# Latent attention of a hybrid layer stack: the softmax denominators of one batch are added on DVE, copies out of PSUM move to ACT, and the end of the first half runs between products of the second

## The chip, the cores and the metric

The kernel runs on one core of one Trainium2 chip. A core has five engines with a queue of their own each: PE (TensorE, matrix products into PSUM), DVE (VectorE), ACT (ScalarE), POOL (GpSimd) and SP (SyncE, which issues DMAs here). An instruction waits at the head of its engine's queue until what it needs is there, and everything behind it waits too. The metric is the device time in microseconds (us) of one execution of the whole kernel.

## The reference, cut to what matters

The kernel computes two layers of mixed blocks on `x` of shape 2 x 1024 x 128 (batch, rows, width), all in float32. Only the first block is touched, a causal attention with 16 heads whose keys and values come out of a latent of 32 numbers per row:

```python
q_blhd = jnp.einsum('bld,dhk->blhk', x_bld, Wq)
latent_bll = jnp.einsum('bld,dc->blc', x_bld, Wkv_down)
k_blhd = jnp.einsum('blc,chk->blhk', latent_bll, Wk_up)
v_blhd = jnp.einsum('blc,chk->blhk', latent_bll, Wv_up)
attn = jnp.einsum('bqhd,bkhd->bhqk', q_blhd, k_blhd) / jnp.sqrt(jnp.asarray(HD, dtype=x_bld.dtype))
mask = (jnp.arange(l)[None, :] <= jnp.arange(l)[:, None])[None, None]
attn = jax.nn.softmax(jnp.where(mask, attn, neg_inf), axis=-1)
y_blhd = jnp.einsum('bhqk,bkhd->bqhd', attn, v_blhd)
return jnp.einsum('bqhd,hdo->bqo', y_blhd, Wout)
```

After it come, for each batch, a spiking feed-forward, a state-space block (a scan along the rows), a linear attention, experts, another attention and experts again.

## The kernel before

The key matrices are folded into the queries and the value matrices into the output, so that each head works on the latent itself: scores are products of 32 numbers, and the weighed sum of a head has 32 numbers per row. Four heads fill the 128 rows of PE's array; the 16 heads are four *chunks* `c` of four heads `j`. Rows are taken in two *halves* of 512 queries; keys in blocks `kb` of 128. A half needs the key blocks 0 to 3, or 0 to 7, and of the four blocks on the diagonal only the queries from the block on: 512, 384, 256 and 128 columns. One pair (c, kb) is a *unit*: 16 units in the first half, 32 in the second, the last four of each chunk diagonal, the others full.

A unit, in `LatentAttention.attend` (L265), has two parts. `exponentials` (L274): four score products of one head each (L282, "scores"), four products that add the negative row maximum to them (L291, "addm"), into two PSUM tiles `a_st` of two heads each; two exponentials on ACT (L301, 1024 elements a row for a full unit) into SBUF tiles `a_pT`, of which there are six; and for a diagonal unit a mask on GpSimd for each tile (L304, `affine_select`). `weigh` (L313): four products with the latent, summed over a chunk's units in the PSUM bank `a_oT` (L320, "weighing"), and four products with ones, summed over a whole half in the bank `a_dT` (L328, "denominators"). At a chunk's last unit DVE copies `a_oT` into SBUF, `a_oU` (L336). The step that computes the exponentials of one unit weighs the unit before.

The *end* of a half follows its last unit: DVE's reciprocal of the denominators (L348), for each chunk a product that spreads them over the rows ("pick", L352) and DVE's multiplication of `a_oU` with it (L353), and for each of four row blocks four output products (L358) that DVE adds to the residual `x_res` (L362). Picks and outputs use `a_st` tiles as well.

Batch 0 runs alone: `first_layer` drains `attend(0)` (three `a_st` tiles of two banks, `a_oT` and `a_dT` one bank each, eight banks in all), and there a scheduler orders each engine's instructions by times that it estimates. Then the maxima of batch 1 (L225, L243) are woven with batch 0's feed-forward (`spiking_steps`, whose norm has a square root on ACT, L66), and `attend(1)`, with two `a_st` tiles, with batch 0's state-space loop: inside `tc.manual_schedule` each engine takes its instructions in the order in which the program writes them. The loop has 32 steps of two loads, a decay on ACT (L606) and three DVE instructions (L637, L638 the scan, L639); `weave` takes 1.75 steps of the generator `attend(1)`, that is as many `yield`s, for each step of the loop:

```python
        attend = latent.attend(1, work, ps, ps_o)
        with tc.tile_pool(name="s_work", bufs=1, reuse_waits="tile") as work:
            weave(space[0].loop(work, bank), attend, 1.75)
        drain(attend)
```

Of the kernel before, what the change touches and what calls it, by code (L numbers as in the profile page):

```python
# [9 lines left out]
F32 = mybir.dt.float32  # L10
BF16 = mybir.dt.bfloat16
AF = mybir.ActivationFunctionType
ALU = mybir.AluOpType
# [4 lines left out]
ALL = {ENG.PE, ENG.DVE, ENG.Activation, ENG.Pool, ENG.SP}  # L18

P = 128  # L20
B = 2
L = 1024
D = 128
NT = B * L // P
TPB = L // P
# [3 lines left out]
class Ctx:  # L29


    def __init__(self, ctx, tc, dram):
        nc = tc.nc
        self.nc, self.tc, self.dram = nc, tc, dram
        self.const = ctx.enter_context(tc.tile_pool(name="const", bufs=1))
        self.small = ctx.enter_context(tc.tile_pool(name="small", bufs=4))
        self.x = self.const.tile([P, NT, D], F32, name="x_res")
        self.ident = self.const.tile([P, P], F32, name="ident")
        make_identity(nc, self.ident)
        self.eps = self.const.tile([P, 1], F32, name="eps")  # L40
        nc.vector.memset(self.eps, EPS)
# [46 lines left out]
def drain(steps):  # L88
    for _ in steps:
        pass  # L90
# [20 lines left out]
class LatentAttention:  # L111
# [3 lines left out]
    C, J, LD = 4, 4, 32  # L115
# [146 lines left out]
        nc.vector.tensor_copy(self.nmT[b], pt.rearrange("p a b -> p (a b)"))  # L262
        yield

    def attend(self, b, work, ps, ps_o):  # L265
        g, nc, C, J = self.g, self.g.nc, self.C, self.J
        qT, latT, lat, nmT = self.qT[b], self.latT[b], self.lat[b], self.nmT[b]
        for half in range(2):
            kbs = list(range(4 * half + 4))
            dT = ps_o.tile([P, 512], F32, name="a0_dT")  # L270
            oU = work.tile([P, C, 512], F32, name="a0_oU")
            oTs = {}

            def exponentials(c, kb):  # L274

                off = max(kb * P - half * 512, 0)
                q0 = half * 512 + off
                n = 512 - off
                ss = [ps.tile([P, 2, 512], F32, name="a0_st") for _ in range(2)]
                for j in range(J):  # L280
                    quad = slice(32 * j, 32 * j + 32)
                    nc.tensor.matmul(  # L282
                        ss[j // 2][:, j % 2, off:],
                        latT[quad, bass.ts(kb, P)],
                        qT[quad, c, q0 : q0 + n],
                        start=True,
                        stop=False,
                    )
                for j in range(J):
                    quad = slice(32 * j, 32 * j + 32)  # L290
                    nc.tensor.matmul(  # L291
                        ss[j // 2][:, j % 2, off:],
                        self.addm[quad, c, :],
                        nmT[quad, q0 : q0 + n],
                        start=False,
                        stop=True,
                    )
                pTs = []
                for s in ss:
                    pT = work.tile([P, 2, 512], F32, name="a0_pT", bufs=6)  # L300
                    nc.scalar.activation(pT[:, :, off:], s[:, :, off:], AF.Exp)  # L301
                    if kb * P >= half * 512:
                        diag = pT[:, :, off : off + P]
                        nc.gpsimd.affine_select(  # L304
                            out=diag,
                            in_=diag,
                            pattern=[[0, 2], [1, P]],
                            compare_op=ALU.is_ge,
                            fill=0.0,
                            base=0,  # L310
                            channel_multiplier=-1,
                        )
                    pTs.append(pT)  # L313
                return pTs, off

            def weigh(c, kb, pTs, off):
                if kb == 0:
                    oTs[c] = ps_o.tile([P, 512], F32, name="a0_oT")
                for j in range(J):
                    nc.tensor.matmul(  # L320
                        oTs[c][32 * j : 32 * j + 32, off:],
                        lat[:, kb, :],
                        pTs[j // 2][:, j % 2, off:],
                        start=(kb == 0),
                        stop=(kb == kbs[-1]),
                    )
                for j in range(J):
                    nc.tensor.matmul(  # L328
                        dT[32 * j : 32 * j + 32, off:],
                        self.ones[:, c, :],  # L330
                        pTs[j // 2][:, j % 2, off:],
                        start=(c == 0 and kb == 0),
                        stop=(c == C - 1 and kb == kbs[-1]),
                    )
                if kb == kbs[-1]:
                    nc.vector.tensor_copy(oU[:, c, :], oTs.pop(c))  # L336

            units = [(c, kb) for c in range(C) for kb in kbs]
            held = {}
            for step in range(len(units) + 1):  # L340
                if step < len(units):
                    held[step] = exponentials(*units[step])
                if step >= 1:
                    weigh(*units[step - 1], *held.pop(step - 1))
                yield

            rec = work.tile([P, 512], F32, name="a0_rec")
            nc.vector.reciprocal(rec, dT)  # L348
            yield
            for c in range(C):  # L350
                rr = ps.tile([P, 2, 512], F32, name="a0_st")
                nc.tensor.matmul(rr[:, 0, :], self.pick[:, c, :], rec, start=True, stop=True)  # L352
                nc.vector.tensor_mul(oU[:, c, :], oU[:, c, :], rr[:, 0, :])  # L353
            yield
            for i in range(4):
                pf = ps.tile([P, 2, 512], F32, name="a0_st")
                for c in range(C):
                    nc.tensor.matmul(  # L358
                        pf[:, 0, :D], oU[:, c, bass.ts(i, P)], self.wvo[:, c, :], start=(c == 0), stop=(c == C - 1)
                    )  # L360
                xt = g.x[:, b * TPB + 4 * half + i, :]
                nc.vector.tensor_add(xt, xt, pf[:, 0, :D])  # L362
            yield

# [829 lines left out]
def first_layer(g, w, open_experts, load_expert):  # L1196

    tc = g.tc
# [12 lines left out]
    with ExitStack() as es:  # L1211
        latent.project([pool(es, "a0_batch0", 1), own])
        with tc.tile_pool(name="a0_seq", bufs=1) as seq, tc.tile_pool(name="a0_ps_a", bufs=2, space=PSUM) as ps:
            drain(latent.row_maxima(0, seq, ps, 4))
        work = pool(es, "a0_work", 2)
        ps, ps_o = pool(es, "a0_ps_b", 3, space=PSUM), pool(es, "a0_ps_o", 1, space=PSUM)
        drain(latent.attend(0, work, ps, ps_o))

    bank = banks(spaces, "bank", 2)
    shared = StateConstants(g, w, pool(spaces, "s_one", 1))  # L1220
# [25 lines left out]
    with tc.manual_schedule(engines=ALL):  # L1246
# [7 lines left out]
        work = pool(latents, "a0_work", 1, **right)  # L1254
# [133 lines left out]
```

## Time and profile before

| | |
|---|---|
| time, median of 3 runs | 2319.74 us (2317.05 to 2331.03) |
| the profiled execution's own time | 2328.53 us |
| its span, first to last instruction | 2326.8 us |
| mean granted PE clock | 0.931 |
| busy: PE, DVE, ACT, POOL | 87%, 70%, 51%, 37% of the span |
| attention of batch 0, half 0, its end, half 1, its end | 147.8 to 198, to 211, to 305, to 319.5 us |
| attention of batch 1, woven with the state-space loop: half 0, its end, half 1, its end | 487 to 544, to 568, to 676, to 694 us |

The profile is one execution, recorded by the hardware. Its views: the page with busy times and the costliest groups of instructions (line, engine, operation, out <- in, shape, count, busy time, mean ns, idle time before and who ended it); the timeline (start, duration, engine, line, operation, in order of time, with neighbours merged); the stretches (busy time of each engine in a window, with the clock that PE was granted, 1.00 being full); one line's instructions with minimum, median and maximum; and the waits (who waited for whom, us in total, times, the longest). A float32 product shows as two records, so a group of four products has eight. A busy PE is not PE at its peak.

### The profile page before, as it was taken

What the parts mean: (1) busy time and instruction counts of PE and PEld (TensorE: products, weight loads), DVE (VectorE), ACT (ScalarE), POOL (GpSimd) and SP (SyncE); (2) the same over time, 40 slices, a digit from 0 to 9 for tenths busy, and PEclk for the clock granted to TensorE, in tenths of its full rate; (3) what the DMA queues carried; (4) which work ended last, traced back from release to release, by engine and by line L of the source; (5) the groups of instructions that cost most, each with busy time, mean ns of one, the idle gap of its engine ahead of it and who ended that gap; (6) DMA issues with size and microseconds to landing.
All of it is one profiled execution on the core that took longest, in us unless ns stands there. A gap on an engine that the chain in (4) does not pass through costs nothing. (4 is left out here: it accounts for less than half of the span.)

```text
span 2326.8 us, 36810 instructions
## 1 busy us (share of the span) xinstructions
PE 2015.9 (87%) x15152; PEld 1184.5 (51%) x15152; DVE 1629.0 (70%) x1988; ACT 1183.5 (51%) x1486; POOL 854.9 (37%) x460
## 2 busy tenths in 40 slices
PE   7779988887987748789698799999977999999999
PEld 4323344323334313235345577677755777777754
DVE  5851047788974659993423699899978999999732
ACT  1014521353643458764322576777735777777632
POOL 0001100033320000000102277878788787877700
PEclk9789997878998879899799899999989999999999
DMA  3000000076732067640000266566556665665500
GB/s 86 1 1 1 2 1 1 18 190 152 185 93 89 4 159 184 162 106 0 1 1 0 64 153 157 145 152 157 146 150 152 157 155 155 153 162 146 137 5 5
DMA packets 72647, 220.19 MB, mean 95 GB/s; under 512 B 9056, under 2 KB 19744, under 8 KB 72352
## 3 DMA queue, kind: packets, MB, share of 16 engines
q1 hardware_dynamic: 53584, 149.40, 21.5%
q0 software_dynamic: 18432, 67.12, 15.3%
q8 instruction: 119, 1.95, 0.3%
q10 hardware_dynamic: 464, 1.33, 0.3%
q14 instruction: 48, 0.39, 0.1%
HBM read 78.35 MB, written 5.24 MB: 36 GB/s over the span
## 5 line engine op out<-in xcount | busy, mean ns | idle before, releaser
L1075 POOL TENSOR_TENSOR h_a<-h_e,h_r 128x2048 f32<-128x2048 f32 x128 | 581.4, 4542 | 130.4 <-PE h_po L1081 93.9
L1041 DVE TENSOR_REDUCE h_m<-h_s 128x128 f32<-128x2048 f32 x128 | 293.2, 2291 | 73.2 <-PE h_s L1030 73.1
L1065 PE MATMUL h_pd<-h_e,ident 128*128 128x128 f32 x2048 | 267.4, 285 | 43.4 <-DMA h_e<-h_e 29.6
L1050 ACT ACTIVATE h_e<-h_e 128x1024 f32<-128x1024 f32 x256 | 256.5, 1049 | 89.6 <-DVE h_e L1047 71.4
L1047 DVE TENSOR_TENSOR h_e<-h_s,h_m 128x2048 f32<-128x2048 f32 x128 | 292.6, 2286 | 3.4 <-DVE h_m L1041 1.7
L1065 PEld LDWEIGHTS h_pd<-h_e,ident 128*128 128x128 f32 x2048 | 244.6, 196 | 87.3 <-DVE x_res L914 41.5
L304 POOL TENSOR_SCALAR_AFFINE_SELECT a_pT<-a_pT 128x256 f32<-128x256 f32 x128 | 97.2, 775 | 431.4 <-ACT a_pT L301 430.5
L301 ACT ACTIVATE a_pT<-a_st 128x1024 f32<-128x1024 f32 (+1 forms) x192 | 145.1, 808 | 139.1 <-PE a_st L291 137.0
L886 ACT ACT_TABLE_LOAD x105 | 134.7, 1283 | 150.5 <-PE e_pgu L879 150.3
L806 DVE TENSOR_TENSOR e_h<-e_sg,e_pu 128x512 f32<-128x512 f32 x128 | 87.0, 686 | 176.5 <-PE e_pu L802 151.2
L243 DVE TENSOR_REDUCE a_nm<-a_s 128x2 f32<-128x1024 f32 (+7 forms) x144 | 168.4, 1218 | 48.5 <-PE a_s L234 24.2
L804 ACT ACTIVATE e_sg<-e_pg 128x512 f32<-128x512 f32 x128 | 76.0, 596 | 192.5 <-PE e_pg L801 192.3
L825 PE MATMUL e_po<-e_h,Wd 128*128 128x512 f32 x256 | 139.4, 630 | 39.4 <-DVE e_h L806 39.3
L225 PE MATMUL a_s<-a_latT,a_qT 32*128 32x512 f32 (+3 forms) x768 | 128.7, 650 | 49.4 <-DVE a_nm L243 47.6
L905 PEld LDWEIGHTS h_pd<-Wd,e_h 128*128 128x128 f32 x1024 | 125.5, 191 | 90.1 <-DVE e_h L894 76.8
L1030 PE MATMUL h_s<-h_qz,h_kT 32*128 32x512 f32 x1024 | 148.5, 649 | 19.5 <-DVE h_e L1047 13.9
L879 PE MATMUL e_pgu<-e_uT,Wg 128*128 128x256 f32 x512 | 154.1, 383 | 4.0 <-ACT h_qz L994 2.1
L905 PE MATMUL h_pd<-Wd,e_h 128*128 128x128 f32 x1024 | 149.1, 287 | 5.9 <-DVE e_h L894 3.7
L879 PE MATMUL e_pgu<-e_uT,Wu 128*128 128x256 f32 x512 | 152.3, 379 | 0.0
L1060 POOL DMA_DIRECT2D h_e<-h_e x128 | 113.6, 887 | 104.0 <-DVE h_m L1041 48.8
L638 DVE TENSOR_TENSOR_SCAN s_h<-s_a,s_h 128x1024 f32<-128x1024 f32 x64 | 147.4, 2303 | 5.9 <-ACT s_a L606 1.7
L801 PE MATMUL e_pg<-e_uT,Wg 128*128 128x512 f32 x256 | 141.9, 638 | 2.1 <-ACT e_uT L794 2.1
(246 smaller groups left out, 3191.6 us busy)
## 6 DMA issues: line engine op xcount, KB each, us to landing
h_e<-h_e SPq DMA_DIRECT2D x128, 512.0 KB, 4.0
h_e<-h_e POOLq DMA_DIRECT2D x128, 512.0 KB, 4.6
s_a<-s_steps SPq DMA_DIRECT2D x64, 512.0 KB, 4.8
s_h<-s_steps SPq DMA_DIRECT2D x64, 512.0 KB, 6.3
s_steps<-s_delta SPq DMA_DIRECT2D x4, 512.0 KB, 2.6
s_steps<-s_dtx SPq DMA_DIRECT2D x4, 512.0 KB, 3.4
Wg<-in_Wg_dram SPq DMA_DIRECT2D x8, 256.0 KB, 6.0
Wu<-in_Wu_dram SPq DMA_DIRECT2D x8, 256.0 KB, 5.9
```

Of the source, the lines that this page charges most:

```text
L243: nc.vector.tensor_reduce(nm[:, half, i, h : h + together], s[:, :, :n], AX.X, ALU.max, negate=True)
L301: nc.scalar.activation(pT[:, :, off:], s[:, :, off:], AF.Exp)
L638: nc.vector.tensor_tensor_scan(h, a, h, 0.0, ALU.mult, ALU.add)
L801: nc.tensor.matmul(pg, w["Wg"][:, e, f], opened[n], start=True, stop=True)
L879: nc.tensor.matmul(pgu[:, k, :], w[name][:, e, f], uT, start=True, stop=True)
L905: nc.tensor.matmul(po[:, t, :], h[:, bass.ts(t, P)], self.w["Wd"][:, e, fc, :], start=(k == 0), stop=(k == 1))
L1030: nc.tensor.matmul(s[:, j, :].rearrange("p (k q) -> p k q", k=K), kTs[b][quad, bass.ts(kb, P)], qzs[b][quad, :, bass.ts(qb, P)], start=Tru ...
L1041: nc.vector.tensor_reduce(m, heads.rearrange("p h q -> p q h"), AX.X, ALU.max)
L1047: nc.vector.tensor_sub(e, heads, m.unsqueeze(1).to_broadcast([P, H, P]))
L1050: nc.scalar.activation(eh, eh, AF.Exp, scale=scale)
L1065: nc.tensor.matmul(pd, g.ident, e2[:, k, :], start=(k == 0), stop=(k == 7))
L1075: nc.gpsimd.tensor_mul(a, e, r.unsqueeze(1).to_broadcast([P, H, P]))
```

## The change

Three things are changed, all in `attend`.

For batch 0 (`added=True`) the denominators' products are not made for each unit. The exponentials of a chunk's unit kb = 0 go into two tiles of their own (`a_sum0`, `a_sum1`), DVE adds those of every later unit of the chunk to them (two `tensor_add` per unit), and `total_denominators` makes one group of four products of 512 columns for a chunk, one step after the chunk's last weighing, behind the weighing of the next chunk's first unit. `attend(0)` is now inside `tc.manual_schedule`, so its order is the written one: four scores, four addm, then the weighing of the unit before. Batch 1 keeps its products with ones.

For both batches ACT instead of DVE copies `a_oT` into `a_oU`, and ACT copies `a_dT` into SBUF before DVE's reciprocal, which then works in place.

For both batches the end of the first half is a generator of its own, whose pieces are taken between the steps of the second half: copy and reciprocal after the first exponentials, then two picks, two picks, two outputs, two outputs, one piece per step, each behind that step's scores and weighing. The end of the second half still follows it. In what the scheduler makes of the program around batch 0, the square root of batch 0's first feed-forward norm (L66 `f_rs`, with a table load on either side) now stands on ACT between the two exponentials of width 384 of the second half's first chunk, where before it stood between the halves.

```diff
+            for step in range(len(units) + 2):
+                if step < len(units):
+                    held[step] = sums.exponentials(*units[step])
+                if step == 0:
+                    next(end, None)
+                if 1 <= step <= len(units):
+                    c, kb = units[step - 1]
+                    if step == 1:
+                        sums.open()
+                    sums.weigh(c, kb, *held.pop(step - 1))
+                if added and step >= 2 and units[step - 2][1] == kbs[-1]:
+                    sums.total_denominators(units[step - 2][0])
+                if step > 0:
+                    next(end, None)
+                yield
+            drain(end)
+            end = sums.end()
+        for _ in end:
+            yield
...
             pTs = []
-                for s in ss:
-                    pT = work.tile([P, 2, 512], F32, name="a0_pT", bufs=6)
+            for k, s in enumerate(ss):
+                if self.added and kb == 0:
+                    pT = self.work.tile([P, 2, 512], F32, name=f"a0_sum{k}")
+                    self.total[c, k] = pT
+                else:
+                    pT = self.work.tile([P, 2, 512], F32, name="a0_pT", bufs=6)
...
+        def total_denominators(self, c):
+            self.denominators(c, [self.total.pop((c, k)) for k in range(2)], 0, c == 0, c == self.latent.C - 1)
...
+            if not self.added:
+                self.denominators(c, pTs, off, c == 0 and kb == 0, c == latent.C - 1 and last)
+            elif kb > 0:
+                for k, pT in enumerate(pTs):
+                    total = self.total[c, k][:, :, off:]
+                    nc.vector.tensor_add(total, total, pT[:, :, off:])
+            if last:
+                if c == 0:
+                    self.oU = self.work.tile([P, latent.C, 512], F32, name="a0_oU")
-                if kb == kbs[-1]:
-                    nc.vector.tensor_copy(oU[:, c, :], oTs.pop(c))
+                nc.scalar.copy(self.oU[:, c, :], self.oTs.pop(c))
...
-            nc.vector.reciprocal(rec, dT)
+            nc.scalar.copy(rec, self.dT)
+            nc.vector.reciprocal(rec, rec)
             yield
             for c in range(C):
...
                 nc.vector.tensor_mul(oU[:, c, :], oU[:, c, :], rr[:, 0, :])
-            yield
+                if c % 2:
+                    yield
             for i in range(4):
...
                 nc.vector.tensor_add(xt, xt, pf[:, 0, :D])
-            yield
+                if i % 2:
+                    yield
...
-        drain(latent.attend(0, work, ps, ps_o))
+        with tc.manual_schedule(engines=ALL):
+            drain(latent.attend(0, work, ps, ps_o, added=True))
```

## The prediction

> **What bounds the kernel now.** I first cut the span into stages, since only two of them contain changed code: batch 0's attention runs from 147.8 to 319.5 us, batch 1's from 487 to 694 us. The view by stretches, core 0 (columns: stretch, its length, busy time of PE, PEld, DVE, ACT, POOL with instruction counts, granted clock, DMA share, GB/s):
>
> ```profile
> 147.80:198.00 50.20, 48.94 (x448) 18.15 (x448) 2.19 (x5) 23.30 (x34) 12.81 (x32) 0.93 0.00 1
> 198.00:211.00 13.00, 9.16 (x46) 5.95 (x48) 8.56 (x16) 0.13 (x1) 0.00 (x0) 0.87 0.00 1
> 211.00:305.00 94.00, 92.53 (x896) 28.94 (x894) 3.01 (x7) 53.50 (x67) 13.02 (x33) 0.98 0.01 1
> 305.00:320.00 15.00, 10.78 (x49) 6.62 (x50) 8.25 (x17) 0.00 (x0) 2.13 (x1) 0.77 0.00 0
> 487.00:544.00 57.00, 48.83 (x476) 18.09 (x478) 49.86 (x33) 33.77 (x45) 39.67 (x32) 0.92 0.95 220
> 544.00:568.00 24.00, 11.67 (x52) 7.49 (x44) 16.70 (x15) 0.00 (x0) 0.00 (x0) 0.72 0.49 116
> 568.00:676.00 108.00, 103.20 (x977) 35.53 (x976) 96.01 (x66) 72.68 (x84) 31.93 (x32) 1.00 0.66 158
> 676.00:694.00 18.00, 12.31 (x52) 7.34 (x56) 11.52 (x12) 0.00 (x0) 0.00 (x0) 0.72 0.00 1
> ```
>
> The reader is to see that batch 0's products (rows 1 and 3) are PE's alone, with DVE idle; that each half's end (rows 2, 4, 6, 8) leaves PE waiting and its clock below 0.9; and that in batch 1 DVE, with the state scan, is nearly as full as PE. The timeline then gives the price of one full unit in steady state, in batch 0's second half:
>
> ```profile
> 246.35 0.39 PE L291 MATMUL a_st<-a_nmT,a_addm 32*128 32x512 bf16 x4
> 246.67 1.06 PE L320 MATMUL a_oT<-a_pT,a_lat 128*32 128x512 f32 x8
> 246.83 1.94 ACT L301 ACTIVATE a_pT<-a_st 128x1024 f32<-128x1024 f32 x2 [1.21 <-PE a_st L291]
> 247.56 1.04 PE L328 MATMUL a_dT<-a_pT,a_ones 128*32 128x512 f32 x8
> 248.53 1.15 PE L282 MATMUL a_st<-a_qT,a_latT 32*128 32x512 f32 x8
> 249.49 0.40 PE L291 MATMUL a_st<-a_nmT,a_addm 32*128 32x512 bf16 x4
> ```
>
> From start to start: addm 0.32, weighing 0.89, denominators 0.97, scores 0.96; together 3.14 us, without a gap. The exponentials start 0.48 after addm and take 0.97 each.
>
> **The change, part by part.**
>
> *Denominators, batch 0.* The same timeline prices the group of L328 for 512, 384, 256 and 128 columns at 0.97, 0.76, 0.55 and 0.33 us. A chunk of the first half holds one of each (2.61), one of the second five full ones and the rest (6.49); eight chunks give 36.4 us. One group of 0.97 per chunk comes back: 7.8. PE loses 28.6 us of work, but the path does not.
>
> In full units a ring is late next: three score tiles, two per unit, so the second pair of scores waits for the previous unit's first exponential. Ring: addm to exponential 0.48, exponential 0.97, hand-over 0.1 (the second pair at 260.74 followed an exponential that ended at 260.64), second pair to addm 0.9. That is 2.45 us, against 2.17 of PE work and 1.94 of ACT. So 3.14 becomes 2.45, 0.69 for each of 20 full units of the second half: 13.8. A chunk's returning denominators fit only into the ring's slack of 0.28, so three chunks lose 0.7 each: **gain 11.7**.
>
> *DVE's additions.* Their nearest rows are two-input ones: L637 with 1253 ns for 1024 elements, L563 with 693 for 512; between them 0.97 for 768, and about 0.41 for 256 (L914). A full unit asks 2.4 to 2.5 of DVE, every 2.45 us: it keeps up just, and DVE is idle there now. They cost nothing as long as they lag by less than three units (six a_pT buffers). But they meet GpSimd. The row of its mask, L304, in batch 0 and then in batch 1:
>
> ```profile
> L304 POOL TENSOR_SCALAR_AFFINE_SELECT a_pT<-a_pT x64: 406/406/408, 152.8 to 303.8; 128x256 f32<-128x256 f32 x64
> L304 POOL TENSOR_SCALAR_AFFINE_SELECT a_pT<-a_pT x64: 401/1360/2387, 491.4 to 674.3; 128x256 f32<-128x256 f32 x64
> ```
>
> Beside a busy DVE it takes 1.36 in the median instead of 0.41. The Trainium skill (SBUF — State Buffer, section "Who interferes with whom") speaks against this change here: a DVE instruction with two SBUF inputs and a GpSimd instruction that reads SBUF exclude each other for a whole instruction. By the rule a mask waits for at most one addition, 1.65 in all; by the row, 1.36; by batch 0's present row, 0.41. I walked both kinds of diagonal stretch with the durations above and 0.2 for a hand-over to and from GpSimd.
> A first-half chunk (all four units diagonal) takes 10.66 now (exponentials at 166.86 and 177.51). After: 9.3 with free masks; 9.9 where the third unit's second mask waits for an addition. I take 9.9: **gain 3.0** in four chunks.
> A second-half chunk's last three units, scores 5 to the next chunk's scores, take 6.55 now (251.68 to 258.23), all PE. After: 5.95 with free masks, 7.1 where each mask waits for the addition already running, 8.05 where a second one slips in. I take 7.3: **loss 3.0** in four chunks; bounds +2.4 and -6.
>
> *Between batch 0's halves.* Now 30.7 us pass from the last weighing (198.1) to the first scores of width 384 (228.85): reciprocal 3.35, picks, products, then cold units. After, on PE in written order: last additions and denominators 1.7; scores 0 and 1, weighing 0 until 4.6; picks wait for exponentials, ACT's copy (0.6) and the reciprocal until 7.6; two picks and their DVE products before scores 2 (9.5), two more after weighing 1, four output products in two pairs; scores 5 at 21.1 after scores 0. f_rs (L66) now stands between two exponentials of width 384, with two table loads of 1.28 and its own 0.30: 2.9, of which about 2.5 shows. Sum 25.3, gain 5.4, of which 3.4 is the five units' 0.69 counted above: **gain 2.0**.
>
> *Batch 0's end* is still alone. Additions 0.7, denominators 0.97, ACT's copy with its hand-over 0.7 are new ahead of the reciprocal; the oU copy (0.69) leaves it: **loss 1.6**.
>
> *Batch 1, copies to ACT.* Eight oU copies (0.69 on DVE, about 0.6 on ACT by L413's row) and two of dT. On ACT the wait for PE stands behind the next unit's exponentials, ahead of later exponentials and decays (L606); those exponentials need scores that PE issues after the same weighing, so nothing is held for long. DVE loses 5.5 of work and the waits of this line:
>
> ```profile
> DVE a_oU L336 <- PE a_oT L320: 10.4, 6, 3.4
> ```
>
> But units come every 3.3 us there (573.03, 576.28), 1.75 of them to one loop step of 4.8 on DVE: the attention's ring sets the pace, and I count 0 for this; bounds -3 (held decays) and +8 (first half, where DVE is 87% busy). No DMA is moved, and GpSimd's and SP's queues keep their order.
>
> *Batch 1, between the halves.* Now 544.3 to 584.7, 40.4 us, to the first scores of width 384: DVE goes through loop step, reciprocal, products, loop step, and PE waits (row 6). After, with two score tiles: reciprocal 549 to 552.4, picks to 554.3, their products behind a loop step at 557.3, scores 2 at 558.1, picks 2 and 3 to 563.6, scores 3 at 563.8, outputs, scores 4 at 569.7, outputs, scores 5 at 575.2: **gain 9.5**. The end (row 8) loses 1.0: copy and hand-over ahead of the reciprocal, and the loop step now between two pairs of products.
>
> Sum: 11.7 + 3.0 - 3.0 + 2.0 - 1.6 + 9.5 - 1.0 = 20.6. The profiled execution took 2328.5 (span 2326.8 and 1.7 around it), 8.8 above the median; the difference should hold for either, so 2319.7 - 20.6, about **2299**.
>
> **The rivals.**
>
> *Masks on the path (slower).* GpSimd's masks lie between exponential and weighing in 32 diagonal units. In batch 1 PE waited for them 20.1 + 8.5 us in 32 units, 0.9 each, beside a DVE at 88%. If each unit pays 1.1 (the first half's share there: 17.7 in 16), that is 35; gains without any mask cost are 11.7 + 5.4 + 2.4 + 2.0 - 1.6 = 19.9, so batch 0 loses 15; with batch 1 bringing nothing, 2335. For it: DVE is nearly full in the second half's last units. Against it: in the first half it is 42% full, and its longest instruction is 1.25, not the scan's 2.3. It decides from 0.6 per diagonal unit.
>
> *Batch 1 gives nothing.* If DVE's loop sets the pace, moving the end only moves its waits: 2299 + 8.5, about 2308. For it: DVE is 87 to 89% busy outside the ends. Against it: PE's 24 us at half load, in which DVE does wait.
>
> *More than I count.* If PE runs ahead (masks free, DVE's waits of 10.4 saved, clock full after the halves): +5.4 in the second half's last units, +2.4 in the first half, +8 in batch 1: 2283.
>
> *The additions do not shorten anything* since ACT or the ring is late: 0 for the 11.7 gives 2311; the ring's terms are measured, so I give it little.
>
> **How the numbers follow.** Forecast 0.46 (2288 to 2308), masks 0.20, batch 1 nothing 0.18, more 0.12, no gain from additions 0.04. The range must leave out no more than 2 in 10: from 2276 to 2325, into the slower case's lower part. A difference under 1% (23 us) is about what this kernel's measurement cannot tell from none. Faster by over 1% (below 2296.5): the larger case and over half of the forecast's lower side, 0.42. Slower by over 1%: the masks' case at its worst, 0.10. The rest 0.48.
>
> **What would show it.** Full units of batch 0 at 2.45 us, exponentials to exponentials; denominators in batch 0 in eight groups, all of 512 columns; masks between 0.41 and 1.65; a first-half chunk at 9.9; scores of width 384 some 25 us after batch 0's first half, and 31 after batch 1's; all else unmoved. I am wrong if full units stay near 3.1, if masks in batch 0 have a median like batch 1's and PE's waits for them exceed 20 us, if DVE lags by whole units so that exponentials wait for a_pT buffers, or if the granted clock in batch 0 falls clearly below the 0.98 of now because PE waits a little in each unit.

## The result, and the profile after

The changed kernel takes 2309.65 us (median of 20 runs, 2304.97 to 2317.45); the kernel before, run beside it, 2324.21 (20 runs, 2314.59 to 2333.81). The ratio is 0.994, 95% interval 0.9926 to 0.9954: 14.6 us faster, between 10.7 and 17.2. The prediction was 2299 from a base of 2319.7, a gain of 20.6.

The profiled execution took 2305.94 us (span 2304.1), against 2328.53 (2326.8) before. These two lie 22.6 apart, 8 more than the medians: the one before is 4.3 above its median, the one after 3.7 below.

The view by stretches of the changed kernel, in the same order as before (batch 0: first half, between the halves, second half, end; then batch 1 likewise; columns: stretch, length, busy time of PE, PEld, DVE, ACT, POOL, granted clock, DMA share, GB/s):

```profile
143.70:185.50 41.80, 38.07 (x346) 13.06 (x348) 17.03 (x24) 23.21 (x36) 18.29 (x32) 0.86 0.01 1
185.50:208.66 23.16, 20.37 (x143) 8.38 (x141) 15.26 (x21) 10.66 (x12) 0.81 (x2) 1.00 0.00 1
208.66:278.50 69.84, 64.84 (x573) 19.96 (x572) 49.43 (x54) 46.15 (x60) 21.75 (x30) 0.98 0.00 1
278.50:294.50 16.00, 10.54 (x52) 6.18 (x48) 10.08 (x17) 1.30 (x3) 2.36 (x1) 0.89 0.00 1
463.40:521.50 58.10, 50.20 (x480) 17.75 (x480) 53.79 (x34) 32.86 (x46) 40.83 (x32) 0.92 1.01 232
521.50:555.50 34.00, 28.86 (x186) 11.09 (x184) 20.78 (x18) 14.72 (x16) 2.62 (x2) 0.90 0.40 93
555.50:652.00 96.50, 88.33 (x836) 29.80 (x834) 83.23 (x55) 62.03 (x76) 41.66 (x30) 1.00 0.68 163
652.00:678.00 26.00, 16.95 (x88) 10.77 (x88) 16.37 (x19) 1.34 (x2) 0.00 (x0) 0.80 0.13 36
```

Batch 1 of the kernel before, cut at the same points:

```profile
487.00:544.30 57.30, 49.12 (x480) 18.22 (x480) 49.93 (x34) 33.77 (x45) 39.67 (x32) 0.92 0.95 221
544.30:584.70 40.40, 28.07 (x182) 12.75 (x180) 32.69 (x27) 12.72 (x13) 0.41 (x1) 0.83 0.55 134
584.70:676.00 91.30, 86.50 (x840) 30.15 (x836) 79.94 (x55) 59.95 (x72) 31.52 (x31) 1.00 0.66 157
676.00:703.00 27.00, 18.89 (x88) 12.69 (x88) 15.67 (x18) 0.00 (x0) 0.00 (x0) 0.75 0.33 108
```

The reader is to see two things. Batch 0 is shorter in its first three rows, 150.8 us from the end of its row maxima to the last x_res add of its attention, 171.7 before: -20.9. Batch 1 has lost 6 us between its halves (34.0 where 40.4 were), but its first and third rows have grown by 0.8 and 5.2, and from the end of its row maxima to the last x_res add of the woven stage it takes 214.6, 216.0 before: -1.4. Between the two batches 169.0 stand where 167.5 stood.

That last add of batch 1's stage is the state-space block's (L664 before, L717 after). The attention's own last add comes ahead of it, 206.4 us after the row maxima before and 210.6 after: `attend(1)` now has 57 yields where it had 56, and its last two output products come behind the loop's last work.

The timeline of one full unit in batch 0's second half (start, duration, engine, line, instruction, idle before):

```profile
225.32 0.39 PE L327 MATMUL a_st<-a_nmT,a_addm 32*128 32x512 bf16 x4
...
225.65 1.06 PE L375 MATMUL a_oT<-a_pT,a_lat 128*32 128x512 f32 x8
225.75 1.94 ACT L341 ACTIVATE a_pT<-a_st 128x1024 f32<-128x1024 f32 x2 [1.44 <-PE a_st L327]
...
226.65 1.30 PE L318 MATMUL a_st<-a_qT,a_latT 32*128 32x512 f32 x8
226.80 4.65 DVE L387 TENSOR_TENSOR a_sum<-a_sum,a_pT 128x1024 f32<-128x1024 f32 x4 [0.76 <-ACT a_pT L341]
...
227.61 0.56 PE L327 MATMUL a_st<-a_nmT,a_addm 32*128 32x512 bf16 x4
228.03 1.94 ACT L341 ACTIVATE a_pT<-a_st 128x1024 f32<-128x1024 f32 x2 [0.34 <-PE a_st L327]
...
230.47 1.94 ACT L341 ACTIVATE a_pT<-a_st 128x1024 f32<-128x1024 f32 x2 [0.50 <-PE a_st L327]
```

The denominators' 0.97 is gone: a unit takes 2.28 to 2.44 us from exponentials to exponentials (225.75, 228.03, 230.47), 3.14 before. Four additions take 4.65, so DVE asks 2.3 of each unit and keeps up. The masks of batch 0 on `a_pT` tiles (eight more are on `a_sum` tiles, at 406 ns each), and then of batch 1 (shortest, median, longest ns):

```profile
L344 POOL TENSOR_SCALAR_AFFINE_SELECT a_pT<-a_pT x56: 401/802/1177, 151.2 to 277.3; 128x256 f32<-128x256 f32 x56
...
L344 POOL TENSOR_SCALAR_AFFINE_SELECT a_pT<-a_pT x64: 401/1384/2386, 467.5 to 648.1; 128x256 f32<-128x256 f32 x64
```

In batch 0 the median has doubled, from 406 to 802 ns, beside DVE's additions.

### The profile page after: what moved, and what is told of

It is laid out like the page before. It is cut to its first block, busy times and chain, and to the rows that moved or that the text cites. A ratio compares the mean times of both kernels' runs of the same rounds, so it can differ in the third digit from the quotient of the medians.

```text
span 2304.1 us, 36329 instructions
## 1 busy us (share of the span) xinstructions
PE 1982.2 (86%) x14832; PEld 1163.1 (50%) x14832; DVE 1694.4 (74%) x2052; ACT 1192.0 (52%) x1506; POOL 884.7 (38%) x460
## 5 line engine op out<-in xcount | busy, mean ns | idle before, releaser
L344 POOL TENSOR_SCALAR_AFFINE_SELECT a_pT<-a_pT 128x256 f32<-128x256 f32 x120 | 122.7, 1044 | 269.7 <-ACT a_pT L341 269.2
L243 DVE TENSOR_REDUCE a_nm<-a_s 128x2 f32<-128x1024 f32 (+7 forms) x144 | 168.2, 1217 | 46.0 <-PE a_s L234 25.3
L341 ACT ACTIVATE a_pT<-a_st 128x1024 f32<-128x1024 f32 (+3 forms) x176 | 130.0, 792 | 103.7 <-PE a_st L327 103.2
L878 PE MATMUL e_po<-e_h,Wd 128*128 128x512 f32 x256 | 138.5, 627 | 40.4 <-DVE e_h L859 40.3
L225 PE MATMUL a_s<-a_latT,a_qT 32*128 32x512 f32 (+3 forms) x768 | 123.3, 622 | 51.5 <-DVE a_nm L243 49.8
L1083 PE MATMUL h_s<-h_qz,h_kT 32*128 32x512 f32 x1024 | 148.1, 648 | 18.8 <-DVE h_e L1100 13.7
L691 DVE TENSOR_TENSOR_SCAN s_h<-s_a,s_h 128x1024 f32<-128x1024 f32 x64 | 147.4, 2303 | 14.6 <-ACT s_a L659 11.1
L1113 POOL DMA_DIRECT2D h_e<-h_e x128 | 114.1, 891 | 109.4 <-DVE h_m L1094 48.7
```

What stands on the lines that cost most here:

```text
L243: nc.vector.tensor_reduce(nm[:, half, i, h : h + together], s[:, :, :n], AX.X, ALU.max, negate=True)
L691: nc.vector.tensor_tensor_scan(h, a, h, 0.0, ALU.mult, ALU.add)
L878: nc.tensor.matmul(po, w["Wd"][:, e, fc, :], hp, start=(e == 0 and fc == 0), stop=last)
L1083: nc.tensor.matmul(s[:, j, :].rearrange("p (k q) -> p k q", k=K), kTs[b][quad, bass.ts(kb, P)], qzs[b][quad, :, bass.ts(qb, P)], start=Tru ...
```

## The experiments

All stages below are measured between the same points as above: batch 0 from the end of its row maxima to the last x_res add of its attention, batch 1 from the end of its row maxima to the last x_res add of the woven stage, whichever of the two chains makes it (the state-space block does in all runs but `b1_end_ahead`). Stages are read from one profile of each kernel. Ratios are to the kernel before, run beside each on the same chip. The planner of the expectations is the scheduler that orders batch 0 before.

### Each batch's part alone

`b0_alone` keeps batch 1's attention in its form before, `b1_alone` batch 0's:

```
-        attend = latent.attend(1, work, ps, ps_o)
+        attend = latent.attend_before(1, work, ps, ps_o)
```

```
-        with tc.manual_schedule(engines=ALL):
-            drain(latent.attend(0, work, ps, ps_o, added=True))
+        drain(latent.attend_before(0, work, ps, ps_o))
```

(`attend_before` is the function of the kernel before under another name.)

> Batch 0's attention as in the changed kernel, batch 1's as before (scheduled code of batch 1 in the form before: copies on DVE, the first half's end ahead of the second half's products). Theory A, all of the gain is batch 0's: batch 0's stage about 151 us (171.7 before), batch 1's about 216, and a total 14 to 20 us under the kernel before, at or below the changed kernel's. Theory B, both parts gain as the prediction summed them (12.1 and 8.5): the total 8 to 12 us under the kernel before, and so 3 to 8 us slower than the changed kernel.

> Batch 1's attention as in the changed kernel (copies on ACT, first half's end between the second half's products), batch 0's as before. Theory A: the boundary between the halves shrinks by about 6 us and the rest of the stage gives it back, so the total stands within 3 us of the kernel before. Theory B, the prediction's own terms: 8.5 us under the kernel before.

`b0_alone`: 2310.33 us, ratio 0.9938 (0.9914 to 0.9962); batch 0's stage 150.5, batch 1's 215.9. `b1_alone`: 2323.82, ratio 0.9998 (0.9981 to 1.0015); stages 172.9 and 214.5. Theory A holds: the gain that the medians show is batch 0's, and batch 1's part, for which the prediction counted 8.5, brings 1.5 us in its stage and nothing that the medians show. Even the 1.5 is not clear: with batch 1 in its form before, the stage took between 211.8 and 216.0 us in five profiles.

### The written order, the copies and the additions, one after the other

`b0_order` is `b0_alone` without the additions; `b0_written_only` is the kernel before with nothing but the written order:

```
-            drain(latent.attend(0, work, ps, ps_o, added=True))
+            drain(latent.attend(0, work, ps, ps_o))
```

```
-        drain(latent.attend(0, work, ps, ps_o))
+        with tc.manual_schedule(engines=ALL):
+            drain(latent.attend(0, work, ps, ps_o))
```

> Batch 0 in the written order, with copies on ACT and its first half's end between the second half's products, but without DVE's additions (PE computes all 36 us of denominators, as before); batch 1 as before. If the additions carry the gain, full units stay at 3.1 us and a first-half chunk near 10.7 us, and only the boundary between the halves gains, 2 to 8 us: 3 to 6 us under the kernel before. If the written order carries it (PE no longer waiting where the planner put instructions in another order), this is 12 us or more under the kernel before.

> The kernel before with one edit: batch 0's attention is issued in the order in which its code is written, and nothing else is changed (denominators on PE, copies on DVE, the first half's end ahead of the second half). Theory O, the planner's order at the start of each chunk (the next but one scores are split around the first weighing, so an exponential starts 1.05 us later) is what the written order takes away: a steady first-half chunk 9.5 to 9.6 us (10.66 before), a second-half chunk 21.8 (22.8 before), the boundary between the halves at 30 us or so, batch 0's stage 162 to 165 us (171.7 before), and a total 6 to 9 us under the kernel before. Rival, the copies on ACT and the interleaved end made the chunks shorter: chunks as before, total within 3 us of the kernel before.

`b0_order`: 2313.28, ratio 0.9948 (0.9930 to 0.9965). `b0_written_only`: 2314.76, ratio 0.9960 (0.9946 to 0.9973). Neither expectation for `b0_order` had it: the full units stayed at 3.1 us as the first said, yet the gain was nearly what the second said. For `b0_written_only` theory O had it nearly to the figure. Batch 0's stage in its parts (us; the landmarks are first exponentials of chunks; the columns between the halves and at the end hold a chunk of units beside the end itself):

| | to 2nd chunk | 2nd to 4th | 4th to 2nd of second half | 2nd to 4th | to last add | stage |
|---|---|---|---|---|---|---|
| before | 19.0 | 21.3 | 48.7 | 45.6 | 37.0 | 171.7 |
| written order alone | 15.8 | 18.8 | 48.1 | 43.2 | 37.2 | 163.2 |
| and copies on ACT, end between products | 16.2 | 19.1 | 42.7 | 43.5 | 36.7 | 158.1 |
| and additions (`b0_alone`) | 14.3 | 18.6 | 43.3 | 39.0 | 35.3 | 150.5 |

The first column also moves with PE's clock: in the first 15 us of the stage the granted clock was 0.77 in the first row and 0.61 to 0.64 in the other three. Of kernels with the same code, the form before took 20.4 there at 0.62 (`b1_alone`), and the changed form 12.1 at 0.88 (`b1_decay2`). The step from the first row to the second is thus rather too small than too large, and the last three rows can be compared.

The written order by itself takes 8.5 us off, where the prediction had no term for it; the medians have 9.4. Where they come from is seen at the start of a chunk. Before, in the timeline of the second half:

```profile
262.00 1.94 ACT L301 ACTIVATE a_pT<-a_st 128x1024 f32<-128x1024 f32 x2 [0.39 <-PE a_st L291]
...
262.02 1.06 PE L328 MATMUL a_dT<-a_pT,a_ones 128*32 128x512 f32 x8
...
263.01 1.12 PE L282 MATMUL a_st<-a_qT,a_latT 32*128 32x512 f32 x2
...
264.06 1.06 PE L320 MATMUL a_oT<-a_pT,a_lat 128*32 128x512 f32 x8
...
266.02 0.39 PE L291 MATMUL a_st<-a_nmT,a_addm 32*128 32x512 bf16 x3
...
266.49 1.94 ACT L301 ACTIVATE a_pT<-a_st 128x1024 f32<-128x1024 f32 x2 [2.56 <-PE a_st L291]
```

and in `b0_written_only`:

```profile
270.10 1.94 ACT L301 ACTIVATE a_pT<-a_st 128x1024 f32<-128x1024 f32 x2 [0.39 <-PE a_st L291]
...
270.12 1.07 PE L320 MATMUL a_oT<-a_pT,a_lat 128*32 128x512 f32 x8
...
271.01 1.04 PE L328 MATMUL a_dT<-a_pT,a_ones 128*32 128x512 f32 x8
...
271.98 1.14 PE L282 MATMUL a_st<-a_qT,a_latT 32*128 32x512 f32 x8
...
272.94 0.39 PE L291 MATMUL a_st<-a_nmT,a_addm 32*128 32x512 bf16 x4
...
273.42 1.94 ACT L301 ACTIVATE a_pT<-a_st 128x1024 f32<-128x1024 f32 x2 [1.38 <-PE a_st L291]
```

The scheduler had put the chunk's first denominators (L328) ahead of its weighing (L320), and one of the third unit's four score products (L282, two instructions of eight) between them. This one product takes 1.12 us by itself, as long as all four take in one piece (1.14). In the written order the next exponential starts 3.32 after the last, in the scheduler's 4.49. A chunk gains 1.2 by it, in the first half (10.66 to 9.42) as in the second (22.82 to 21.61); at the end of the stage the written order gives 1.4 back (37.0 to 37.2, with a chunk's 1.2 in it). In neither timeline does PE wait in this stretch, so the rows of PE's waits could not show it. ACT's wait did (2.56 for PE, against 1.38), and the reason stood in the order of PE's lines.

The copies on ACT and the interleaved end then take 5.1 off, nearly all between the halves (48.1 to 42.7). The additions in place of the products take 7.6 off: 2.2 for each steady second-half chunk (21.73 to 19.51), 0.2 for a first-half one (9.53 to 9.32), the rest in the first chunk and in the last. These two steps are seen in the traces only. By the medians, each to the kernel before, `b0_order` is 11.5 us faster and `b0_alone` 14.4, and their intervals overlap: that the additions by themselves make the whole kernel faster is not shown by the medians.

### What the additions cost

`b0_noadds` leaves them out, and takes the denominators from each chunk's first key block alone:

```
-            elif kb > 0:
-                for k, pT in enumerate(pTs):
-                    total = self.total[c, k][:, :, off:]
-                    nc.vector.tensor_add(total, total, pT[:, :, off:])
```

> As b0_alone, but DVE's 56 additions of batch 0 are left out; the denominators are then taken from the first key block of each chunk alone, so the output is not the reference's. Measures what the additions cost where they are. If they only delay masks: masks in batch 0 return to 0.41 us each (x56: 401/802/1177 ns beside the additions), PE's 30 us of waits for masks fall by about half, and the second half's last three units fall from 6.8 to 6.0 us; in all 5 to 8 us under b0_alone. If the additions cost nothing, as the prediction took it for full units: within 2 us of b0_alone.

There are 80 additions, 24 in the first half and 56 in the second, and all are left out. 2300.97 us, ratio 0.9901 (0.9881 to 0.9922), 9.4 under `b0_alone` by the medians; batch 0's stage 143.6, 7 under. A steady second-half chunk takes 18.58 (19.51 with additions), a first-half one 8.88 (9.32). The masks:

```profile
L444 POOL TENSOR_SCALAR_AFFINE_SELECT a_pT<-a_pT x56: 406/406/408, 153.7 to 272.6; 128x256 f32<-128x256 f32 x56
```

All are back at 406 ns. PE's waits for masks on `a_pT` fall from 26.3 us (20.3 at the weight load, 6.0 at the product) to 10.0; 3.7 for those on `a_sum` stay. So the additions are not free: they give back 7 of the 14.5 us (158.1 - 143.6) that PE's relief from the products is worth without them. By the landmarks of the table they cost 0.3, 0.9, 2.7, 1.9 and 1.1. How much of it is the masks' and how much is PE waiting for sums was not separated; between the halves (2.7) the root of the next experiment stands in another place, too.

### The root between the exponentials

The prediction named a root (f_rs, L66) that the scheduler puts between two exponentials. `one_section` issues the attention of batch 0 and what follows it as one written stretch, so the root comes behind it:

```
-        with tc.manual_schedule(engines=ALL):
-            drain(latent.attend(0, work, ps, ps_o, added=True))
+        sections.enter_context(tc.manual_schedule(engines=ALL))
+        drain(latent.attend(0, work, ps, ps_o, added=True))
...
-    with tc.manual_schedule(engines=ALL):
+    with sections:
```

> The changed kernel, with batch 0's attention and what follows it issued as one stretch of written order, so that the feed-forward's first root (L66, with two table loads) no longer stands between exponentials of width 384 in batch 0's second half; it comes behind the attention, with its statistics on DVE (4 x 0.44 us). The prediction counted 2.5 us for it where it stood: batch 0's stage 2 to 3.5 us shorter than 150.8, the middle stage 3 to 5 us longer than 169.0, the total within 3 us of the changed kernel.

2303.96, ratio 0.9927 (0.9906 to 0.9949). ACT's timeline in the changed kernel:

```profile
209.77 0.82 ACT L341 ACTIVATE a_pT<-a_st 128x768 f32<-128x768 f32 x1 [2.06 <-PE a_st L327]
210.61 1.28 ACT L66 ACT_TABLE_LOAD   x1
211.90 0.30 ACT L66 ACTIVATE f_rs<-f_mv,eps 128x4 f32<-128x4 f32 x1
212.22 1.28 ACT L341 ACT_TABLE_LOAD   x1
...
220.04 1.94 ACT L341 ACTIVATE a_sum<-a_st 128x1024 f32<-128x1024 f32 x2 [3.07 <-PE a_st L327]
```

and in `one_section`:

```profile
209.76 1.51 ACT L341 ACTIVATE a_pT<-a_st 128x768 f32<-128x768 f32 x2 [2.06 <-PE a_st L327]
...
216.09 1.94 ACT L341 ACTIVATE a_sum<-a_st 128x1024 f32<-128x1024 f32 x2 [2.08 <-PE a_st L327]
```

The same first exponential of width 384 stands at 209.77 and 209.76, the next chunk at 220.04 and 216.09: 2.86 us of instructions on ACT cost 3.95 on the path. Batch 0's stage is 146.2, 4.6 shorter (0.7 of it in the last chunk and the end), the middle, from there to the end of batch 1's row maxima, 170.3, 1.2 longer: less comes back than was expected, and 3.4 stay, which is too little for the medians to show.

### Three moves in batch 1

`b1_decay2` issues each decay a loop step earlier; `b1_copies_dve` puts batch 1's oU copies back on DVE; `b1_end_ahead` puts its first half's end back ahead of the second half:

```
+            near = 2 if b == 0 else 1
-            if t + 1 < len(tiles):
-                decay(t + 1, ahead[0][0])
+            if t + near < len(tiles):
+                decay(t + near, ahead[near - 1][0])
```

```
-                nc.scalar.copy(self.oU[:, c, :], self.oTs.pop(c))
+                (nc.scalar.copy if self.added else nc.vector.tensor_copy)(self.oU[:, c, :], self.oTs.pop(c))
```

```
             end = sums.end()
+            if not added:
+                yield from end
```

> The changed kernel, with each decay of the state loop beside batch 1's attention issued one loop step earlier on ACT (two steps ahead of its scan, not one). Theory H, copies on ACT hold the decays and the scan then waits: the scan's waits for decays in this stage fall from 11.1 to 3 us or less, and batch 1's stage from 214.6 to 205 to 210 us, total 4 to 9 us under the changed kernel. Rival, the stage's pace is set by DVE and PE together elsewhere (units come when PE gets exponentials): the waits for decays go, others take their place, and the stage stays within 3 us of 214.6.

> The changed kernel with batch 1's eight copies of the weighed latents back on DVE (ACT keeps the denominators' copies, and the first half's end stays between the second half's products). Theory H: DVE's waits for decays fall to about 2 us, DVE's waits for the weighing (10.4 us before) come back, the stage stays at 213 to 217 us. The prediction's own step (copies worth 0, bounds -3 to +8) has it within 3 us of the changed kernel too; a stage under 210 would say that moving the copies was a loss by itself.

> The changed kernel with batch 1's first-half end put back ahead of the second half's first scores (copies stay on ACT). If the interleaved end brings the 6 us by which the boundary was seen to shrink, batch 1's stage is 4 to 7 us longer than 214.6. If the stage's length is set by the state loop on DVE, the boundary grows to 40 us again and the stage stays within 2 us of 214.6.

The times: 2307.47 (ratio 0.9934, 0.9908 to 0.9959), 2307.45 (0.9937, 0.9908 to 0.9966) and 2306.43 (0.9924, 0.9898 to 0.9951). Batch 1's stage: 214.4, 214.6 and 214.5, and 214.6 in the changed kernel. DVE's waits in this stage (us in total, times, longest), in the changed kernel:

```profile
DVE s_h L691 <- ACT s_a L659: 11.1, 8, 2.0
DVE a_oU L404 <- PE a_st L403: 10.6, 4, 7.2
DVE a_rec L399 <- ACT a_rec L398: 4.8, 1, 4.8
```

in `b1_decay2`:

```profile
DVE a_oU L404 <- PE a_st L403: 9.3, 4, 6.0
DVE a_rec L399 <- ACT a_rec L398: 9.2, 2, 7.0
DVE s_h L694 <- ACT s_a L659: 7.6, 6, 2.0
```

and in `b1_copies_dve`:

```profile
DVE a_oU L391 <- PE a_oT L375: 13.7, 7, 3.7
DVE a_oU L404 <- PE a_st L403: 9.3, 4, 6.0
...
DVE s_h L691 <- ACT s_a L659: 0.2, 1, 0.2
```

The copies on ACT do hold the decays, as theory H says: with them on DVE, the scan's 11.1 us of waits for decays shrink to 0.2. But then DVE waits 13.7 for the weighing, and the stage is the same to a tenth. Theory H falls as a cause of the stage's length: the wait that is taken away comes back in another place.

`b1_decay2` says less than it was meant to. Only 3.5 us leave the scan, and 4.4 come to the reciprocal; and ACT's second decay, which waits for its load, now stands ahead of the attention's first exponentials, which start 7.8 us after the row maxima instead of 3.0. The stage is 0.2 shorter nevertheless.

The interleaved end is worth nothing to the stage either: with the end ahead, the first exponential of width 384 in batch 1's second half starts 10 us later, counted from the row maxima (103.8, against 93.3), and the stage is as long. But another chain ends it. The loop's last add comes 5.3 us earlier than in the changed kernel (209.2, 214.6), the attention's 4.0 later (214.5, 210.6). With the end ahead `attend(1)` has 62 yields and not 57, so that `weave` lets the loop get ahead of it, too: one chain gains what the other loses, and that the two stages are equal is partly chance.

### The state loop and batch 1's attention, each alone

`b1_apart` runs batch 1's attention first and the state loop after it:

```
+        drain(attend)
         with tc.tile_pool(name="s_work", bufs=1, reuse_waits="tile") as work:
-            weave(space[0].loop(work, bank), attend, 1.75)
-        drain(attend)
+            drain(space[0].loop(work, bank))
```

> The changed kernel, with all of batch 1's attention put ahead of the state loop that lies beside it (no work left out). Gives each one's own length: the attention alone, estimated from batch 0's first four measured landmarks as about 165 us (172.9 in batch 0's old form, with two score tiles here and not three), and the loop alone, 32 steps of 4.8 us of DVE work and 1 MB of loads each at the 233 GB/s seen (4.5 us), 155 to 165 us. If the loop alone needs 190 us or more, it sets batch 1's stage of 214.6; if both need about 160, the stage is two chains of waits that share DVE and ACT, and neither part of the change can shorten it alone. Total about 100 to 120 us over the changed kernel.

2422.38 us, ratio 1.0437 (1.0404 to 1.0471). The view by stretches, the attention and then the loop:

```profile
461.50:626.00 164.50, 151.78 (x1424) 57.28 (x1424) 14.41 (x18) 83.00 (x111) 25.62 (x64) 0.95 0.08 18
626.00:793.80 167.80, 77.96 (x160) 14.21 (x160) 155.71 (x106) 33.44 (x29) 0.00 (x0) 0.55 0.85 213
```

Each needs about 165 us alone: the attention is PE's (151.8 of 164.5), the loop DVE's (155.7 of 167.8). Woven they take 214.6, in which PE is busy for 184.4 (in part at a lower clock) and DVE for 174.1. Neither engine is full, and neither chain alone sets the length. That the two wait for each other where they share DVE and ACT is the reading that fits the three moves above; it is argued from them, and not shown by itself. A rival is untested: `weave` fixes how the two are mixed in each engine's queue, and no other ratio than 1.75 was tried.

### The mask on PE

`mask_pe` adds the causal mask to the scores on PE, in both batches, and has no mask on GpSimd:

```
+            if kb * P >= half * 512:
+                for j in range(J):
+                    nc.tensor.matmul(
+                        ss[j // 2][:, j % 2, off : off + P],
+                        latent.mask,
+                        latent.identb,
+                        start=False,
+                        stop=False,
+                    )
...
-                    nc.gpsimd.affine_select(
...
```

> The changed kernel, with the causal mask of both batches' attention added by PE into the scores (a product of the bf16 mask of the row maxima with a bf16 identity, four of 128 columns per diagonal unit, estimated at 0.2 to 0.3 us per unit from the 0.23 us that the four addm products of 128 columns take) in place of GpSimd's 128 masks. Theory: in batch 0 the wait exponential-mask-weighing goes and DVE's additions delay nothing any more; the stage falls from 150.8 to 143 to 148 us (143.6 was the stage without additions, with masks at 0.41 us). In batch 1 PE's waits for masks (41 us in sum) vanish; if those waits pace the stage it falls from 214.6 to 190 to 200 us; if the state loop's DVE work and loads pace it, it stays at 208 to 214. Total 7 to 20 us under the changed kernel.

2304.52, ratio 0.9931 (0.9911 to 0.9951). Batch 1's stage falls to 207.3: PE's 40.7 us of waits for masks (29.4 at the weight load, 11.3 at the product) are gone, and 7.3 us are gained: a little more than where the loop paces the stage (208 to 214 expected), far less than where the masks do (190 to 200). Batch 0's rises to 156.2: the mask lies on PE, which has the more work of the two there.

```profile
176.61 0.40 PE L327 MATMUL a_st<-a_identb,a_mask 128*128 128x128 bf16 x4
176.94 0.29 PE L336 MATMUL a_st<-a_nmT,a_addm 32*128 32x256 bf16 x4
```

The four mask products take 0.33 from start to start. A first-half chunk of four diagonal units is 0.37 longer (9.69, against 9.32), a second-half one 0.25 shorter. Between the halves another 3.1 are lost: the scheduler put the root's table load ahead of its statistics there, and ACT waited 2.75 us for those.

### Both gains together

`both` is `one_section` with the mask on PE in batch 1 alone (the condition above with `and not self.added`, and GpSimd's with `and self.added`).

> The changed kernel with the two edits that were seen to shorten a stage: batch 0's attention and what follows it in one stretch of written order, and batch 1's masks (only those) added by PE into the scores. If the two gains add: batch 0's stage 146 us, the middle 170, batch 1's stage 207, together about 11 us under the changed kernel (7.3 of it from batch 1, 3.3 from batch 0 and the middle), a ratio to the kernel before of 0.988 to 0.990. If batch 1's 207 was a run's chance (the same code of batch 1 stood between 211.8 and 216.0 in other runs), 3 us under the changed kernel, ratio 0.992 to 0.993.

2301.55 us, ratio 0.9910 (0.9891 to 0.9929). Batch 0, the middle and batch 1 in the view by stretches:

```profile
148.23:295.13 146.90, 132.83 (x1104) 47.56 (x1104) 87.94 (x100) 79.74 (x109) 43.86 (x65) 0.94 0.01 1
295.13:465.20 170.07, 142.84 (x688) 61.53 (x688) 126.86 (x208) 43.40 (x64) 3.24 (x2) 0.80 0.07 21
465.20:672.50 207.30, 186.77 (x1712) 74.46 (x1712) 169.56 (x123) 111.37 (x139) 0.00 (x0) 0.92 0.68 161
```

Their sum, 524.3, is 10.1 below the changed kernel's 534.4: the stage gains add. The median is the lowest of all kernels here that add up whole denominators; its interval still overlaps that of the changed kernel a little (0.9926 to 0.9954). The 0.988 to 0.990 that the stages gave lies at the interval's lower end.

## Why the prediction was right in its sum, and where it was wrong

The sign, the size within 6 us and the range were right. That the sum came so near is partly luck: its terms were wrong in both directions, and partly cancelled: batch 0's share was 12.1 and measured 20.9, batch 1's was 8.5 and measured 1.4.

- **Full units, 3.14 to 2.45.** Right in mechanism and size: 2.28 to 2.44. The ring is there: the second pair of scores at 226.82 and the scores at 229.09 follow exponentials that end at 226.77 and 229.05. With the loss in the last three units, the prediction had (11.7 - 3.0) / 4 = 2.18 per second-half chunk; the additions by themselves bring 2.22 in a steady one (21.73 to 19.51). In the chunk between the halves they bring nothing (42.7 to 43.3), though 3.4 of the 11.7 were counted there. That chunk's gain is the interleaved end's, 5.4 (48.1 to 42.7) where 2.0 were counted.
- **The start of each chunk: the term that was missing.** "3.14 us, without a gap" is a unit from the middle of a chunk. The prediction multiplied it, and saw neither that a chunk's start cost 1.2 more nor why: the scheduler's order on PE. The written order alone shortens the stage by 8.5 us, nearly the whole of batch 0's surplus (20.9 - 12.1 = 8.8).
- **First-half chunk, 10.66 to 9.9, gain 3.0.** Measured 9.32, but of these 1.34 the written order has 1.24. With the order seen, the additions' gain there is 0.2 per steady chunk, and 1.9 in the first one, which runs at a lower clock (0.61 and 0.63 in the first 15 us of `b0_order` and `b0_alone`).
- **Second half's last three units.** Predicted 7.3 from scores 5 to the next chunk's scores, measured 6.79 in the steady chunks (6.55 before) and 5.76 without additions, where it had 5.95 with free masks. The masks cost something there, less than was taken.
- **The rule on shared ports.** By the Trainium skill (SBUF — State Buffer, section "Who interferes with whom") a DVE instruction with two SBUF inputs contends with a GpSimd instruction that reads SBUF; the prediction drew from it that a mask waits for at most one addition. No mask in batch 0 took more than 1.18, which is within 0.41 + 1.24 (the mean of a full addition), and the whole price of the additions, 7 us, is far from the 35 that the masks' rival took from batch 1. It is near the 7.8 that the prediction had for all masks (2.4 in the first half, 5.4 in the second), though 2.7 of it lie between the halves, where it had none. The rule was a better guide than batch 1's row, where masks of up to 2.39 stand beside a scan of 2.3. Still, half of one sign of being wrong came true: PE's waits for masks in batch 0 are 26.3 us, above the 20 named, with a median mask of 0.80.
- **Between batch 0's halves, 30.7 to 25.3.** Measured 23.2 to the first scores of width 384; the root fell just behind this point, and without its 2.5 the prediction had 22.8. The root was mis-sized: 2.5 counted, 3.95 measured.
- **Batch 0's end, loss 1.6.** Measured 14.8 to 16.0: 1.2. The written order by itself costs 1.4 there (above), so the reason given, the copies and the hand-over, is not shown to be the right one.
- **Batch 1's copies, 0.** Right in the sum; the held decays, which the prediction dismissed ("nothing is held for long"), are there with 11.1 us of the scan's waits, and cost nothing, since DVE's waits for the weighing went.
- **Batch 1 between the halves, gain 9.5: the step that failed.** 6.3 were gained where they were counted (40.4 to 34.1) and were lost again behind it: the last chunk's first exponential of width 384 is 3.7 earlier than before, counted from the row maxima (175.8, 179.5), the reciprocal 0.4 later (189.3, 188.9). The prediction valued a wait of PE as if PE's chain set the stage, and the stage kept 1.4 of the 8.5. The rival "batch 1 gives nothing" was right, and its gain of 12.1 is nearer to 14.6 than the forecast's 20.6; its reason was not: DVE's loop does not set the pace alone (about 165 us by itself, 214.6 in the stage).

What stays open: the batches' stages and the middle between them lose 20.8 us in the two traces, the medians 14.6. Outside them lie stretches that no edit touched, the start (141.8 to 148.2 us in the profiles of all kernels here) and the 1,620 us after batch 1 (1623.4 to 1630.9). They vary between profiles by as much as what is sought, and whether the change moves them was not tried. Why batch 1's stage takes 214.6 where each chain needs 165 is open too.

## What to carry to other kernels

Before pricing a change to a loop, read one whole period of the engine that bounds it, its irregular turn too, and not only the steady unit: here the scheduler's order at each chunk's start held more than the copies did, and no wait of that engine showed it. Where two chains share engines, a wait taken from one of them is not a gain until the other is shown to have slack: run each alone, and ask which of them ends the stage. An idle engine that takes over work is not free when its instruction and another engine's stand in each other's way: price both.

## What was not expected of the hardware

A root of 0.30 us between two exponentials cost 3.95 on the path with its two table loads of 1.28. Four bf16 mask products of 128 rows and 128 columns took 0.33 us, as long as the four addm products of 32 rows and 512 columns (0.32) and twice those of 32 rows and 128 columns (0.16, from 178.71 to 178.87 in `mask_pe`). And one of four score products of 32 rows, issued apart from the others, took 1.12 us, the time of all four together.
